# A feed-forward's second product by seven block products instead of eight, with its buffers moved and its gathers placed earlier in the loop

## The chip, the cores and the metric

The kernel runs on one core of one Trainium2 chip. TensorE (PE) multiplies, and loads its stationary operand with an instruction of its own (shown as PEld); VectorE (DVE), ScalarE (ACT) and GpSimd (POOL) do the element-wise work; SyncE (SP) issues most of the transfers, and POOL issues the indirect ones. Each engine works through its own queue in order. The metric is the device time of the core in microseconds (us), as the median of several runs. Beside it stands one profiled execution, from which all durations come.

## The reference

The input is one sequence of S = 4096 tokens of D = 256 features, in float32. It is normalised once, and the result goes two ways.

```python
xn = _layernorm(x)
x  = x + attn_block(xn) + experts(xn)

# attn_block: attention in windows of 64 with 8 heads, then
x = xn + attn;  x = _layernorm(x, gamma, beta)
h = gelu(x @ W1 + b1)            # W1: 256 x 1024
x = x + (h @ W2 + b2)            # W2: 1024 x 256

# experts: 8 experts with 816 hidden features, the best two of each token
h = silu((xf @ gw.T + gb) * (xf @ uw.T + ub))
acc = acc + w[:, None] * (h @ dw.T + db)
```

The change is in `h @ W2`, the feed-forward's second product.

## The kernel before

The constants are P = 128, D = 256, F1 = 1024, FC1 = F1 / P = 8, G = 512 tokens in a group, NG = 8 groups, TG = 4 tiles of 128 tokens in a group, B = 256. Everything is float32. For TensorE, PE, DVE, ACT, POOL and SP the order of work is the order in which the code is written: nothing reorders it.

The kernel has three stretches. First the tokens are normalised, projected and routed to experts. Then 34 expert units, of two tiles of tokens or one, run in a loop whose first 32 turns also carry the attention; five further units follow that run only if the routing has need of them (`whole`, L890). Each unit's results go to a table in DRAM, `done`. In the third stretch, from L1267 to the end, the feed-forward runs over eight groups of 512 tokens. In the profiled execution it begins near 867 us.

For a group g the third stretch has these steps:

- `second_loads` (L1040): SP loads the attention's output `x2` and the input `acc`, each 128 x 1024.
- `second_norm` (L1047): DVE normalises `x2` (four instructions at L1051) and multiplies by gamma (L1059); POOL adds beta to `x2` (L1060), `b2` to `acc` (L1061) and `x2` to `acc` (L1062).
- `turned2` (L1064): PE transposes `x2` with eight instructions (L1069); DVE copies the two results to `x2T` (L1072).
- `hidden` (L1075): 16 products with 512 moving columns (L1080), two for each of eight chunks f; ACT applies gelu with the bias (L1087) and writes the tile `hT` of 128 x 8 x 512.
- `picked` (L1090): POOL issues eight indirect gathers (L1096), for four tiles of tokens the results of two experts each, from `done` into eight buffers `got`.
- `combined` (L1105): DVE adds each gathered tile to `acc`, times the token's share (L1109): eight instructions.
- `second` (L1113): 32 products with 256 moving columns (L1118), each summing over the eight chunks f; DVE adds the results to `acc`, two tiles at once (L1125).
- `store` (L1128): SP writes `acc` to the output (L1129).

A product in float32 is two MATMUL instructions with a weight load ahead of each, so a group's `hidden` has 32 MATMULs in the profile, and its `second` has 64. The stationary operand of `second` is a 128 x 128 piece of `hT`, and the moving one a row of `W2`.

The loop from L1273 sets the order. In the turn of g: `hidden(g)`, `turned2(g + 1)`, loads and `second_norm(g + 2)`, `second(g - 1)`, `combined(g - 1)`, `store(g - 1)`, `picked(g)`. After the loop come `combined(7)`, and `second(7)` with a store after each half. PSUM has seven banks in turn (`bank`, L124; `psm`, L115); `ph`, `pt`, `pd` all draw on it.

SBUF is dealt out from two sides as a stack. On the left lie the constants, and the experts' pools `wexp` (L113) and `he` (L789), which are kept to the end. On the right, the attention's pools are given back at L1184, and in their place come `wf` (the weights), `hf` (x2T and hT, two buffers each), `accp`, `got`, and `late` (what the last five units need: gathered tokens, their transposes, two sets of weights).

## Time and profile before

| | |
|---|---|
| three runs, us | 1101.41, 1103.53, 1105.42 (median 1103.53) |
| profiled execution, us | 1102.41 |
| its span, first to last instruction, us | 1100.7 |
| granted TensorE clock | 1.000 of full speed |
| busy: PE, PEld, DVE, ACT, POOL, us | 1084.8, 868.7, 591.3, 495.3, 502.7 |
| L1118 MATMUL (`pd`), 128x256, x512 | 111.7 us in all |
| L1080 MATMUL (`ph`), 128x512, x256 | 111.3 us in all |
| L1069 MATMUL (`pt`), 128x128, x64 | 8.3 us in all |

How to read it: "busy" is the time in which at least one instruction of the engine was under way. MATMULs are pipelined, so the mean length of one (379 ns for `pd`) is more than the distance from one to the next; the distance is a stretch's length over its count. A share of busy time over the whole kernel mixes stretches with different limits; the change touches the third one, which is looked at by itself. The profiled execution's device time is 1.7 us above its span.

### The profile page before, as it was taken

How to read it: one execution, taken by the hardware profiler on the slowest of the kernel's cores; microseconds unless marked ns; L12 is line 12 of the kernel's file. 1: busy time of each engine (PE TensorE's matmuls, PEld its weight loads, DVE VectorE, ACT ScalarE, POOL GpSimd, SP SyncE). 2: the span in 40 equal slices, each digit the busy share in tenths (PEclk: the TensorE clock that was granted, in tenths of full speed). 3: DMA queues.
4: the chain of work that ended last, by engine and by line, in shares of the span. 5: the costliest groups of instructions: out<-in, count | busy, mean ns of one | idle time of the engine just before them, and what ended most of it. 6: DMA issues, size and time to landing. Idle time of an engine off the chain costs nothing. (4 is left out here: it accounts for less than half of the span.)

```text
span 1100.7 us, 18039 instructions
## 1 busy us (share of the span) xinstructions
PE 1084.8 (99%) x6424; PEld 868.7 (79%) x6424; DVE 591.3 (54%) x1571; ACT 495.3 (45%) x1170; POOL 502.7 (46%) x620
## 2 busy tenths in 40 slices
PE   8998999999999999999999999999999999999998
PEld 6577888887888888888888888888888666666667
DVE  6655656657566566665666666656433233323213
ACT  4526446544555546646555564465343321111110
POOL 6425544455445443654455445534213175555422
PEclk9999999999999999999999999999999999999999
DMA  9152445545445354454544554545575323333112
GB/s 291 61 234 73 139 136 172 180 141 156 152 147 194 119 187 148 170 163 155 193 149 138 179 182 140 169 150 197 176 265 205 120 77 96 96 96 96 57 58 77
DMA packets 60748, 163.37 MB, mean 148 GB/s; under 512 B 6288, under 2 KB 46608, under 8 KB 51184
## 3 DMA queue, kind: packets, MB, share of 16 engines
q1 hardware_dynamic: 54176, 144.48, 37.7%
q0 software_dynamic: 6480, 17.70, 6.2%
q8 instruction: 52, 0.85, 0.3%
q14 instruction: 40, 0.33, 0.1%
HBM read 140.28 MB, written 21.89 MB: 147 GB/s over the span
## 5 line engine op out<-in xcount | busy, mean ns | idle before, releaser
L830 PE MATMUL gu<-xsT,wg 128*128 128x256 f32 (+1 forms) x1632 | 357.4, 369 | 0.7 <-ACT xsT L822 0.7
L830 PEld LDWEIGHTS gu<-xsT,wg 128*128 128x128 f32 x1632 | 288.6, 190 | 46.2 <-DVE oT L1018 10.3
L838 ACT ACTIVATE gs<-gu,wg 128x256 f32<-128x256 f32 (+1 forms) x204 | 92.1, 454 | 291.3 <-PE gu L830 290.0
L958 POOL TENSOR_TENSOR pr<-pr 128x256 f32<-128x256 f32 x128 | 92.9, 726 | 253.6 <-ACT pr L946 253.6
L874 PE MATMUL pe<-wd,hT 128*128 128x256 f32 x896 | 199.0, 379 | 0.0
L839 DVE SCALAR_TENSOR_TENSOR hT<-gu,wg,gs 128x256 f32<-128x256 f32 (+1 forms) x204 | 95.0, 467 | 177.4 <-ACT gs L838 177.2
L874 PEld LDWEIGHTS pe<-wd,hT 128*128 128x128 f32 x896 | 170.1, 190 | 22.8
L959 POOL TENSOR_TENSOR pr<-pr,ident 128x256 f32<-128x256 f32 x128 | 126.2, 986 | 10.0
L946 ACT ACTIVATE pr<-pr,nm 128x256 f32<-128x256 f32 x256 | 126.8, 498 | 0.4
L1087 ACT ACTIVATE hf<-ph,b 128x512 f32<-128x512 f32 x64 | 44.0, 687 | 158.2 <-PE ph L1080 158.2
L1080 PE MATMUL ph<-x2T,W 128*128 128x512 f32 x256 | 111.3, 593 | 0.8 <-DVE x2T L1072 0.8
L1118 PE MATMUL pd<-W,hf 128*128 128x256 f32 x512 | 111.7, 379 | 0.0
L1118 PEld LDWEIGHTS pd<-W,hf 128*128 128x128 f32 x512 | 96.9, 190 | 13.3 <-issue 0.5
L931 DVE CUSTOM_DVE_ANT_0 pr<-ps,mask 128x256 f32<-128x256 f32 x256 | 90.8, 420 | 23.2 <-PE ps L917 23.2
L804 POOL DMA_INDIRECT xs<-xnd,token x71 | 68.8, 969 | 64.9 <-DVE paired_tiles L771 31.1
L1096 POOL DMA_INDIRECT got<-done,slot x64 | 63.3, 989 | 73.9 <-DVE acc L1109 61.2
L1080 PEld LDWEIGHTS ph<-x2T,W 128*128 128x128 f32 x256 | 48.5, 190 | 58.9 <-issue 56.8
L869 ACT ACTIVATE hT<-hT 128x512 f32<-128x512 f32 (+3 forms) x148 | 80.4, 543 | 7.6 <-DVE hT L839 4.2
L1060 POOL TENSOR_TENSOR x<-x,beta 128x1024 f32<-128x1024 f32 x8 | 18.8, 2350 | 94.4 <-DVE x L1059 94.4
L1125 DVE TENSOR_TENSOR acc<-pd,acc 128x512 f32<-128x512 f32 x16 | 11.0, 690 | 83.3 <-PE pd L1118 83.3
L978 DVE TENSOR_TENSOR pr<-pr,rec 128x1024 f32<-128x1024 f32 x32 | 39.2, 1225 | 27.7 <-POOL pr L958 27.7
L946 ACT ACT_TABLE_LOAD x31 | 39.8, 1283 | 27.5 <-DVE nm L931 27.5
(209 smaller groups left out, 1393.6 us busy)
## 6 DMA issues: line engine op xcount, KB each, us to landing
wg<-in_gate_up SPq DMA_DIRECT2D x37, 1670.5 KB, 7.1
wd<-in_down SPq DMA_DIRECT2D x37, 1024.0 KB, 5.9
done<-y SPq DMA_DIRECT2D x30, 256.0 KB, 2.2
x<-in_x SPq DMA_DIRECT2D x8, 512.0 KB, 5.6
xnd<-xn SPq DMA_DIRECT2D x8, 512.0 KB, 5.4
res<-xnd SPq DMA_DIRECT2D x16, 256.0 KB, 2.9
x1d<-res SPq DMA_DIRECT2D x16, 256.0 KB, 2.2
x<-x1d SPq DMA_DIRECT2D x8, 512.0 KB, 5.8
```

Of the source, the lines that this page charges most:

```text
L804: nc.gpsimd.indirect_dma_start(out=x[:, t, :], out_offset=None, in_=xnd, in_offset=bass.IndirectOffsetOnAxis(ap=token[:, i : i + 1], axis=0),)
L830: nc.tensor.matmul(pb[:, k, :], w[:, lo : lo + P], xT[:, c, :], start=(c == 0), stop=(c == DC - 1),)
L838: nc.scalar.activation(gs, pb[:, 0, :], AF.Identity, bias=w[:, gb : gb + 1])
L839: nc.vector.scalar_tensor_tensor(hT[:, f, :], pb[:, 1, :], w[:, ub : ub + 1], gs, ALU.add, ALU.mult)
L869: nc.scalar.activation(hT[on, lo:hi, :], hT[on, lo:hi, :], AF.Silu)
L874: nc.tensor.matmul(pd[:, t, :], hT[:, f, t * P : (t + 1) * P], w[:, f * D : (f + 1) * D], start=(k == 0), stop=(k == FCE - 1),)
L931: nc.vector.tensor_tensor_reduce(out=pr[:, hh, j, :], in0=ps[hh][:, j, :], in1=mask[:, kind + j, :], scale=-1.0, scalar=-LOWEST, op0=ALU.a ...
L946: nc.scalar.activation(pr[:, hh, j, :], pr[:, hh, j, :], AF.Exp, bias=nm[:, j, hh : hh + 1], scale=-1.0, accum_out=sums[:, j, hh : hh + 1],)
L958: nc.gpsimd.tensor_tensor(first, first, second, ALU.add)
L959: nc.gpsimd.tensor_tensor(second, second, bcast(ident, 2, 1), ALU.mult)
L1080: nc.tensor.matmul(ph, W1[:, c, f * P : (f + 1) * P], x2T[:, c, :], start=(c == 0), stop=(c == DC - 1),)
L1118: nc.tensor.matmul(pd[:, u, :], hT[:, f, (t + u) * P : (t + u + 1) * P], W2[:, f, :], start=(f == 0), stop=(f == FC1 - 1),)
```

## The change

`second` is rewritten. Per group the hidden matrix is a 512 x 1024 matrix and W2 is 1024 x 256; each is cut in two along both sides, into A11..A22 (256 tokens x 512 hidden features) and B11..B22 (512 x 128 features). In place of eight block products, seven are formed, of sums of blocks. Each product has two tiles of tokens, four chunks f and 128 moving columns.

- Sums of W2's blocks: `sums_of_weights`, four POOL instructions, once, into a new tile `V2` (in turn 33 of the unit loop).
- Sums of the hidden blocks: `sums_of_hidden`, per group one POOL instruction and three on DVE, of 128 x 1024 each, into a new tile `hv`.
- The products' results are added to quarters of `acc`, on DVE, by way of a small tile `u` that holds partial sums; ACT copies the first product into it.
- The turn's order is changed: `combined(g - 1)` comes right after `hidden(g)`, `picked(g)` before the products, the sums of the hidden blocks after the second product, loads and `second_norm(g + 2)` after the fifth, the store at the turn's end.
- `wexp`, `he` and `late` are given back after the last unit, and `hf` and `got` are made then, in their place. `late` thus lies directly after `accp` before that.

```diff
-    wexp = pool(ctx, "wexp", bufs=2)
+    experts_done = ctx.enter_context(ExitStack())
+    wexp = pool(experts_done, "wexp", bufs=2)
...
-    he = pool(ctx, "he", bufs=2)
+    he = pool(experts_done, "he", bufs=2)
...
+    FH = FC1 // 2
+    F_LO, F_HI = slice(0, FH), slice(FH, FC1)
+    C1, C2 = slice(0, P), slice(P, D)
+
+    def sums_of_weights():
+        b11, b12, b21, b22 = W2[:, F_LO, C1], W2[:, F_LO, C2], W2[:, F_HI, C1], W2[:, F_HI, C2]
+        t1, t2, t3, t4 = (V2[:, k] for k in range(4))
+        for out_, left_, right_ in ((t1, b12, b11), (t2, b22, t1), (t3, b22, b12), (t4, b21, t2)):
+            nc.gpsimd.tensor_tensor(out_, left_, right_, ALU.subtract)
+
+    def sums_of_hidden(g, hT):
+        v = hf.tile([P, 4, FH, B], F32, tag="hv", name=f"hv{g}")
+        a11, a12, a21, a22 = hT[:, F_LO, 0:B], hT[:, F_HI, 0:B], hT[:, F_LO, B:], hT[:, F_HI, B:]
+        s1, s2, s3, s4 = (v[:, k] for k in range(4))
+        nc.gpsimd.tensor_tensor(s3, a11, a21, ALU.subtract)
+        nc.vector.tensor_tensor(s1, a21, a22, ALU.add)
+        nc.vector.tensor_tensor(s2, s1, a11, ALU.subtract)
+        nc.vector.tensor_tensor(s4, a12, s2, ALU.subtract)
+        return v
...
-    def second(g, acc, hT):
-        for t in range(0, TG, 2):
-            pd = halves(bank(f"pd{g}_{t}"))
-            for u in range(2):
-                for f in range(FC1):
...
-            nc.vector.tensor_tensor(acc[:, t : t + 2, :], pd, acc[:, t : t + 2, :], ALU.add)
-            yield t
+    def second(g, acc, hT, v):
+
+        t1, t2 = slice(0, 2), slice(2, 4)
+        u = hf.tile([P, 2, P], F32, tag="u", name=f"u{g}")
+
+        def product(n, left, right):
+            pb = bank(f"s{g}_{n}").rearrange("p (t n) -> p t n", n=P)[:, 0:2]
+            for t in range(2):
+                for f in range(FH):
                     nc.tensor.matmul(
+                        pb[:, t, :],
+                        left[:, f, t * P : (t + 1) * P],
+                        right[:, f, :],
                         start=(f == 0),
+                        stop=(f == FH - 1),
                     )
+            return pb
+
+        def add(t, cols, pb):
+            nc.vector.tensor_tensor(acc[:, t, cols], pb, acc[:, t, cols], ALU.add)
+
+        p1 = product(1, hT[:, F_LO, 0:B], W2[:, F_LO, C1])
+        nc.scalar.copy(u, p1)
+        add(t1, C1, u)
+        yield
+        p2 = product(2, hT[:, F_HI, 0:B], W2[:, F_HI, C1])
+        add(t1, C1, p2)
+        yield
+        p6 = product(6, v[:, 1], V2[:, 1])
+        nc.vector.tensor_tensor(u, p6, u, ALU.add)
+        add(t1, C2, u)
+        yield
+        p5 = product(5, v[:, 0], V2[:, 0])
+        add(t1, C2, p5)
+        add(t2, C2, p5)
+        yield
+        p7 = product(7, v[:, 2], V2[:, 2])
+        nc.vector.tensor_tensor(u, p7, u, ALU.add)
+        add(t2, C1, u)
+        add(t2, C2, u)
+        yield
+        p3 = product(3, v[:, 3], W2[:, F_HI, C2])
+        add(t1, C2, p3)
+        yield
+        p4 = product(4, hT[:, F_HI, B:], V2[:, 3])
+        add(t2, C1, p4)
+        yield
...
-            hf = pool(ctx, "hf", right, bufs=2)
             accp = pool(ctx, "accp", right, bufs=4)
-            got = pool(ctx, "got", right, bufs=8)
+            V2 = wf.tile([P, 4, FC1 // 2, P], F32, tag="V2", name="V2")
...
-            late = pool(ctx, "late", right)
+            late = pool(late_done, "late", right)
...
         if b == STEPS + 1:
+            sums_of_weights()
...
+    late_done.close()
+    experts_done.close()
+    hf = pool(ctx, "hf", right, bufs=2)
+    got = pool(ctx, "got", right, bufs=8)
     x2T = turned2(0, x2s[0][1])
     second_norm(1, *x2s[1])
...
     for g in range(NG):
         hT = hidden(g, x2T)
+        if g > 0:
+            acc = x2s.pop(g - 1)[0]
+            combined(g - 1, acc, ys)
         if g + 1 < NG:
             x2T = turned2(g + 1, x2s[g + 1][1])
+        ys = picked(g)
+        outs = second(g - 1, acc, *last) if g > 0 else iter(())
+        some(outs, 2)
+        last = hT, sums_of_hidden(g, hT)
+        some(outs, 3)
         if g + 2 < NG:
             x2s[g + 2] = second_loads(g + 2)
             second_norm(g + 2, *x2s[g + 2])
+        some(outs, 2)
         if g > 0:
-            acc = x2s.pop(g - 1)[0]
-            list(second(g - 1, acc, before))
-            combined(g - 1, acc, ys)
             store(g - 1, 0, TG, acc)
-        before = hT
-        ys = picked(g)
     acc = x2s.pop(NG - 1)[0]
     combined(NG - 1, acc, ys)
-    for t in second(NG - 1, acc, before):
-        store(NG - 1, t, 2, acc)
+    outs = second(NG - 1, acc, *last)
+    some(outs, 6)
+    store(NG - 1, 0, 2, acc)
+    some(outs, 1)
+    store(NG - 1, 2, 2, acc)
```

More of the change, by code (lines that the diff above doesn't have):

```diff
@@ L1111, in combined @@
             )
-    def second(g, acc, hT):
-        for t in range(0, TG, 2):
-            pd = halves(bank(f"pd{g}_{t}"))
-            for u in range(2):
-                for f in range(FC1):
+    def second(g, acc, hT, v):
[5 more added lines that the diff above has]
+                for f in range(FH):
                     nc.tensor.matmul(
-                        pd[:, u, :],
-                        hT[:, f, (t + u) * P : (t + u + 1) * P],
-                        W2[:, f, :],
+                        pb[:, t, :],
+                        left[:, f, t * P : (t + 1) * P],
+                        right[:, f, :],
                         start=(f == 0),
-                        stop=(f == FC1 - 1),
+                        stop=(f == FH - 1),
                     )
-            nc.vector.tensor_tensor(acc[:, t : t + 2, :], pd, acc[:, t : t + 2, :], ALU.add)
-            yield t
+            return pb
[27 more added lines that the diff above has]
+        yield
     def store(g, t, n, acc):
@@ L1141, in block_kernel @@
     flags = {}
+    late_done = ctx.enter_context(ExitStack())
     def load_unit(b):
@@ L1267, in block_kernel, with some @@
     x2s[1] = second_loads(1)
+    late_done.close()
+    experts_done.close()
+    hf = pool(ctx, "hf", right, bufs=2)
+    got = pool(ctx, "got", right, bufs=8)
     x2T = turned2(0, x2s[0][1])
     second_norm(1, *x2s[1])
-    before = None
+    last = None
+    def some(steps, n):
+        for _ in range(n):
+            next(steps, None)
     for g in range(NG):
         hT = hidden(g, x2T)
+        if g > 0:
+            acc = x2s.pop(g - 1)[0]
+            combined(g - 1, acc, ys)
         if g + 1 < NG:
             x2T = turned2(g + 1, x2s[g + 1][1])
+        ys = picked(g)
[3 more added lines that the diff above has]
+        some(outs, 3)
         if g + 2 < NG:
```

## The prediction

> **What bounds it now.** I read the summary first, then the chain of work that ended last in order of time, then the stretch it lies in.
>
> ```profile
> PE 1084.8 (99%) x6424; PEld 868.7 (79%) x6424; DVE 591.3 (54%) x1571; ACT 495.3 (45%) x1170; POOL 502.7 (46%) x620
> ```
>
> PE is never idle for long, so time is won only by giving PE less to do. The chain (start us, us, what) shows a loop that is PE alone:
>
> ```profile
> 858.65 5.36 PE whole L830 x48
> ...
> 912.23 13.73 PE ph L1080 x32
> 925.96 0.87 PE pt L1069 x8
> 926.84 13.82 PE pd L1118 x64
> 940.65 13.73 PE ph L1080 x32
> ...
> 1096.03 0.06 DVE acc L1125
> ```
>
> A turn is 13.73 + 0.87 + 13.82 = 28.4 us, without a gap. How full the other engines are in one turn is shown by the busy times of this stretch (length, then PE, PEld, DVE, ACT, POOL, clock, DMA share, GB/s):
>
> ```profile
> 926.80:954.40 27.60, 27.60 (x99) 18.27 (x98) 8.34 (x17) 4.81 (x7) 14.95 (x11) 1.00 0.31 96
> ```
>
> DVE and ACT have two thirds of a turn free, POOL nearly half.
>
> **The products.** Before, `pd` is 64 MATMULs of 256 columns in 13.82 us: 215.9 ns each. After, there are 7 products x 2 tiles x 4 chunks x 2 instructions = 112 MATMULs of 128 columns. Columns fall to 7/8, but each MATMUL still has its own weight load, so loads rise from 64 to 112 a group. The nearest row is the last conditional unit, where 48 MATMULs of just this shape follow each other (durations in ns: min/median/max):
>
> ```profile
> L830 PEld LDWEIGHTS whole<-xsT,wg x48: 191/192/193, 858.4 to 863.6; 128*128 128x128 f32 x48
> L830 PE MATMUL whole<-xsT,wg x48: 274/275/276, 858.5 to 863.7; 128*128 128x128 f32 x48
> ```
>
> The chain gives these 48 as 5.36 us: 111.7 ns each, although one load is recorded as 192 ns; so loads and MATMULs overlap, and the record's length isn't the price. A group costs 112 x 0.1117 = 12.51 us, which saves 1.31 us, and over eight groups **10.5 us**. The lower bound of a MATMUL's price is the transposes, 8 in 0.87 us = 108.8 ns, nearly what half of 215.9 gives: 12.2 us a group, 13 us saved. For the upper one, a fresh bank for each product may cost up to 0.06 us, half a MATMUL: 12.9 us a group, 7.2 us saved.
>
> A rule speaks against this. The Trainium skill, "TensorE: Matmul & The Clock Gate", section "The mechanism", says that a weight load overlaps matmuls in flight only where the row group differs; here all 128 rows are the same. With that page's load price ("LDWEIGHTS", columns over 1.2 GHz: 107 ns) on top of 108.8 ns, a group is an estimated 112 x 0.216 = 24.2 us, 83 us more in all. But then `pd` would now need 64 x (107 + 213) ns = 20.5 us and not 13.82. I take the row.
>
> **DVE.** Its prices, and POOL's:
>
> ```profile
> L1059 DVE TENSOR_TENSOR x<-x,gamma 128x1024 f32<-128x1024 f32 x8 | 9.8, 1225 | 0.3
> L907 DVE TENSOR_TENSOR xs<-whole,wd 128x256 f32<-128x256 f32 x2 | 0.8, 425 | 4.5 <-PE whole L874 2.3 <-PEq L1262 2.3
> L1060 POOL TENSOR_TENSOR x<-x,beta 128x1024 f32<-128x1024 f32 x8 | 18.8, 2350 | 94.4 <-DVE x L1059 94.4
> L1096 POOL DMA_INDIRECT got<-done,slot x64 | 63.3, 989 | 73.9 <-DVE acc L1109 61.2 <-issue 12.5
> ```
>
> Removed: two adds of 128x512, 1.38 us. Added: three sums at 1.225 = 3.68 us, eleven adds of 128x256 at 0.425 = 4.7 us. DVE goes from 8.4 to about 15.4 us in a turn of 27.1: still hidden. Counted from a turn's start T (its `hidden`): `combined` runs from T + 1.4 to 5, the copies of `turned2` at T + 14.2, the sums T + 18.6 to 22.3, gamma ends at T + 27.7, the last add at T + 28.5. What PE needs first of these are the x2T copies (by T + 27.1, ready at T + 15.5) and the banks: `ph` of the next turn takes the bank of the third product at T + 35.7, whose add ends at T + 28.1. No PE wait. Without this cover each late us of DVE would cost a us, but 7 are spare.
>
> **ACT.** One copy of 128x256, 0.37 us as in the row of that shape at L304, without a table load (L304 has none). Hidden: ACT idles 15 us while `pd` runs.
>
> **POOL and the moved gathers.** Eight gathers took 10.06 us (893.95 to 904.01) whether early or late in the turn. With s3 at 2.35 us and three adds of `second_norm` POOL has 10.1 + 4 x 2.35 = 19.5 us in 27.1. In steady state the gathers run from T + 7.7 to 17.8, s3 to 20.2, and beta waits for gamma at T + 27.7, ready long before the `turned2` that needs it, at T + 40.8. `picked` is now queued ahead of s3 and `second_norm`; it waits for `combined(g - 1)`, finished by T + 5, so nothing stands behind it for long. The loads on SP come before the store as queued, and `x2` lands about T + 8, needed at T + 25. The four sums of W2 cost 4 x 1.27 us (L1024's 128x512 row) near 803.4, where POOL is idle until 828.04. All hidden.
>
> **One place is not hidden**: the first turn. There `picked(0)` and s3 now stand before the beta of `second_norm(2)`:
>
> ```profile
> 880.11 2.36 POOL L1062 TENSOR_TENSOR acc<-acc,x 128x1024 f32<-128x1024 f32 x1
> ...
> 896.95 0.14 PEld L1069 LDWEIGHTS pt<-ident,x 128*128 128x128 f32 x1 [0.24 <-issue]
> ```
>
> POOL is free at 882.5. The gathers end at 892.6, s3 at 895.0, beta at 897.4, where PE wants `x2(2)` for its transposes at 896.95. To this comes that POOL is held up by DVE instructions with two SBUF inputs:
>
> ```profile
> 773.87 1.23 DVE L978 TENSOR_TENSOR pr<-pr,rec 128x1024 f32<-128x1024 f32 x1 [1.39 <-POOL pr L958]
> ...
> 773.91 1.76 POOL L959 TENSOR_TENSOR pr<-pr,ident 128x256 f32<-128x256 f32 x1
> ```
>
> (0.72 us elsewhere); a gather beside L1059 took 1.28 in place of 0.95 us. The three sums and gamma stretch the gathers by 4 x 0.33 us: beta ends about 898.9, and PE waits **+1.5 us**, once (0 with no stretch; +3.5 if every DVE sum holds POOL for its whole length). The Trainium skill, "SBUF — State Buffer", section "Who interferes with whom", goes further than the row: whichever of the two starts first blocks the other, so a POOL add of 2.35 us can hold DVE too, which no row here shows. In a turn that is at most four POOL adds, 9.4 us later for DVE: `combined` then ends at T + 39 instead of 32, before the next x2T copies at T + 41.3. Either way the sum stays.
>
> **Memory given back.** `hf` takes the place of `late`, whose last tile is stored to `done` at 867.62, landing 2.2 us later; x2T(0) was written at 867.51. If x2T lies over that tile, the start slips by 2.3 us; over weights or transposes, by 0, as PE's reads are over. `hT` over it costs nothing (gelu begins at 870.28, and seven banks buffer it). `late` is made in the order weights, tokens, so I take 0 and keep 2.3 for the range.
>
> **The tail.** Now PE ends at 1095.70, DVE is still at `combined(7)` because its gathers waited for `combined(6)`; the two adds end at 1097.22, the last store is issued, and the span ends 3.5 us later. After, `combined(7)` is over long before, and after PE's end one add of 0.425 us remains: 0.45 + 3.5 instead of 5.0: **-1.1 us** (-0.5 to -1.5).
>
> **Sum**: -10.5 + 1.5 - 1.1 = -10.1 us. Span 1100.7 - 10.1 = 1090.6; with 1.7 us around it, 1092.3. The profiled execution lies 1.1 us under the median of the runs shown, which would give 1093.4; I put the forecast between, **1092.9**.
>
> **Rivals.** (a) *Weight loads set the pace*, chance 0.07. A load recorded as 192 ns is longer than the 109 ns of MATMUL that must cover it; with hT and acc traffic it might not be covered as in the row. Break-even is 13.82 / 112 = 123 ns a MATMUL; from 128 ns the kernel is slower by over 0.3%. At the recorded 192 ns: 21.5 us a group, +61 us, about 1163. Against: 48 in 5.36 us with PEld busy throughout. (b) *POOL becomes the bound*, 0.06. Its 19.5 us plus all of DVE's two-input work in a turn (gamma 1.2, sums 3.7, adds of `u` 1.7, `combined` 3.9) is 30.0 us against 27.1; six turns give +17 us less some 8 us of lead: about no change, 1102. Against: half of that DVE work falls where POOL waits. (c) *Small waits*: x2T(0) behind the store and a longer first wait, or 0.4 us in each group: 1095 to 1099, chance 0.12. (d) *Nothing is saved because something else ends last*: excluded by a chain that is PE in every turn. The forecast has 0.75.
>
> **From cases to numbers.** 0.3% is 3.3 us, about what this kernel's measurement can tell from no change. Faster: forecast, (c), and a part of (b), 0.88. Same: 0.03 from (b). Slower: (a) and the rest of (b), 0.09. Low end: 13 us from the products, no first wait, tail -1.5: about 1089. High end: products 7.2, first wait 3.5, slip 2.3, tail -0.5 leaves -1.9; not all together, so 1099, which holds (c).
>
> **What would show it.** Right: a group's seven products as 112 MATMULs in 12.5 us, directly after `pt`; PE without idle except near 897 us, then waiting for POOL's beta; after PE's last MATMUL one add. Wrong: gaps of PE between products that wait for DVE (banks) or POOL (s3); a distance of MATMULs above 120 ns; x2T(0) waiting for a transfer.

## The result, and the profile after

The changed kernel took 1098.85 us (median of 9 runs, 1096.73 to 1100.21) beside 1103.05 us (9 runs, 1101.41 to 1105.42) for the kernel before: a ratio of 0.996, 95% interval [0.9948, 0.9972]. It is faster by 4.2 us, where 10.1 us had been predicted; the time, 1098.85 us, lies just inside the range given. The profiled execution of the changed kernel took 1100.01 us with a span of 1098.3 us, so it is read against the 1100.7 us of before: 2.4 us less.

The engines' summary of the profile after. PE has more instructions and 4.7 us less to do, DVE 100 us more:

```profile
PE 1080.1 (98%) x6808; PEld 873.9 (80%) x6808; DVE 691.6 (63%) x1667; ACT 498.1 (45%) x1178; POOL 528.4 (48%) x632
```

The chain that ended last, in order of time (start us, us, what), shows where the gain is and where it went:

```profile
901.53 12.51 PE s L1150 x112
914.04 13.73 PE ph L1081 x32
...
984.24 0.87 PE pt L1070 x8
985.11 7.04 PE s L1150 x63
992.14 0.14 issue
992.29 0.68 PE s L1150 x4
992.97 0.72 issue
993.69 5.29 PE s L1150 x45
998.98 13.73 PE ph L1081 x32
...
1069.58 25.03 PE s L1150 x224
1094.61 0.02 issue
1094.63 0.42 DVE acc L1160
```

In the first turn the seven products take the 12.51 us that were predicted, and the last two groups take 25.03 us. But in the turns between them PE stops inside the products ("issue": it waits for nothing that the profile shows). From the first MATMUL of `s` to the first of the next `ph`, these five turns take 13.52, 13.72, 13.87, 14.12 and 13.53 us, together 6.2 us above 5 x 12.51; some of that lies inside the pieces, whose single records aren't all there. The two timelines of the turn at 985 us show what runs beside it (start us, us, engine, line, operation, idle time before it); first POOL, from the first gather to s3:

```profile
982.28 0.98 POOL L1124 DMA_INDIRECT got<-done,slot  x1
...
991.39 0.94 POOL L1124 DMA_INDIRECT got<-done,slot  x1 [0.30 <-issue]
992.35 2.36 POOL L1112 TENSOR_TENSOR hv<-hf 128x1024 f32<-128x1024 f32 x1
```

Then DVE, with the adds of the first and the second product:

```profile
987.34 0.42 DVE L1160 TENSOR_TENSOR acc<-u,acc 128x256 f32<-128x256 f32 x1 [1.34 <-ACT u L1163]
992.27 0.43 DVE L1160 TENSOR_TENSOR acc<-s,acc 128x256 f32<-128x256 f32 x1 [4.51 <-remote]
```

A product takes 1.79 us, so the second one, begun 1.79 us after 985.11, was done at 988.7. Its add starts at 992.27, 3.6 us later, though DVE idles in front of it. The eighth gather ends at 992.33; within 0.1 us the signal of the second product has arrived and PE, which stopped at 992.14, goes on for four MATMULs, then stops for 0.72 us more. In the other four turns the same add starts 2.7, 3.1, 2.6 and 3.6 us after its product is done, and PE's stops lie between 2.4 us before and 1.5 us after the end of the last gather. So where a row of gathers runs beside the products, PE's signals come late, and PE itself stops.

The third stretch as a whole, from the first `ph` to PE's end, took 227.4 us before (868.26 to 1095.70) and takes 223.2 us (871.38 to 1094.61): -10.5 from the products, +6.2 from these stops; PE's first wait for POOL added nothing in this execution (from that first `ph` to the first product it is 30.15 us in both).

The stretch also begins 3.1 us later. Of this, 1.7 us is one piece of 3.41 us at half the granted clock, at 94.5 us, which this profile has and the profile of before has not (the mean clock is 0.998 here, 1.000 there). 1.65 us is lost in the last attention unit, where PE shows the same kind of stop (16 MATMULs take 5.37 us and not 3.72):

```profile
787.12 0.97 PE L831 MATMUL gu<-xsT,wg 128*128 128x256 f32 x2
788.44 1.19 PE L831 MATMUL gu<-xsT,wg 128*128 128x256 f32 x3 [0.35 <-issue]
789.85 2.64 PE L831 MATMUL gu<-xsT,wg 128*128 128x256 f32 x11 [0.22 <-issue]
```

and again a row of gathers ends just then, at 788.40 us; this is the last of seven, which fetch the conditional units' tokens:

```profile
787.46 0.94 POOL L805 DMA_INDIRECT xs<-xnd,token  x1 [0.30 <-issue]
```

In the kernel before these seven ran from 794.86 to 803.35 us, because the place of `late` made them wait for the attention's store of `res` to `x1d`:

```profile
794.86 0.99 POOL L804 DMA_INDIRECT xs<-xnd,token  x1 [17.02 <-DMA x1d<-res]
```

In the changed kernel they run from 779.91 to 788.40.

At the end one add is left after PE, as forecast: 1098.3 - 1094.61 = 3.7 us, 5.0 before. Sum against the span of before: -10.5 + 6.2 + 3.1 - 1.3 = -2.5 us, against -2.4 measured.

### The profile page after: what moved, and what is told of

It is laid out like the page before. It is cut to its first block, busy times and chain, and to the rows that moved or that the text cites. A ratio compares the mean times of both kernels' runs of the same rounds, so it can differ in the third digit from the quotient of the medians.

```text
span 1098.3 us, 18954 instructions
## 1 busy us (share of the span) xinstructions
PE 1080.1 (98%) x6808; PEld 873.9 (80%) x6808; DVE 691.6 (63%) x1667; ACT 498.1 (45%) x1178; POOL 528.4 (48%) x632
## 5 line engine op out<-in xcount | busy, mean ns | idle before, releaser
L1137 DVE SCALAR_TENSOR_TENSOR acc<-got,share,acc 128x256 f32<-128x256 f32 x64 | 66.7, 1072 | 1.1
L980 DVE TENSOR_REDUCE same<-pr 128x8 f32<-128x1024 f32 x32 | 39.1, 1221 | 19.8 <-POOL pr L960 19.8
L1150 PE MATMUL s<-V,hv 128*128 128x128 f32 x384 | 46.5, 276 | 3.7 <-issue 3.4
```

What stands on the lines that cost most here:

```text
L1150: nc.tensor.matmul(pb[:, t, :], left[:, f, t * P : (t + 1) * P], right[:, f, :], start=(f == 0), stop=(f == FH - 1),)
```

## The experiments

They ran on five chips, called A to E here; the kernels of one chip share their runs of the kernel before. Which chip gave the result is not on record. The chips turned out to matter, so the table names them. "Stops" is the time by which the stretches of the second product in turns 1 to 5 exceed 5 x 12.51 us (5 x 13.82 with eight products), by the profile. "First ph" is the start of the third stretch. Both are of one execution, which need not be a typical one: e1's profile took 1110.73 us and e8's 1099.77 us, each several us above the median of its runs. Pieces at half the granted clock also move "First ph", by up to 1.7 us each.

| kernel | chip | median, us | ratio to before [95%] | stops, us | first ph, us |
|---|---|---|---|---|---|
| changed (result) | - | 1098.85 | 0.9960 [0.9948, 0.9972] | 6.2 | 871.4 |
| e1, changed | A | 1104.76 | 1.0007 [0.9991, 1.0024] | 6.9 | 876.0 |
| e2, `got` made first | A | 1105.43 | 1.0015 [0.9999, 1.0030] | 7.2 | 875.2 |
| e3, gathers last | A | 1109.76 | 1.0055 [1.0037, 1.0073] | 7.1 | 872.1 |
| e4, memory alone | A | 1107.47 | 1.0027 [1.0020, 1.0033] | 0 | 874.3 |
| e9, changed | B | 1098.10 | 0.9951 [0.9932, 0.9970] | 2.8 | 872.2 |
| e6, gathers first | B | 1099.58 | 0.9968 [0.9956, 0.9980] | 0.6 | 870.9 |
| e7, e6 and old place | B | 1097.37 | 0.9948 [0.9935, 0.9961] | 1.0 | 868.0 |
| e8, eight gathers | B | 1095.00 | 0.9921 [0.9907, 0.9935] | 0 | 876.3 |
| e5, `late` in old place | C | 1097.53 | 0.9947 [0.9929, 0.9964] | 4.2 | 869.6 |
| f1, gathers beside eight | C | 1102.36 | 0.9989 [0.9981, 0.9998] | 0 | 869.2 |
| f2, pairs | C | 1102.31 | 0.9993 [0.9981, 1.0004] | 0 | 873.3 |
| f3, pairs and old place | C | 1100.10 | 0.9971 [0.9959, 0.9983] | 0 | 868.8 |
| f4, pairs from turn 1 | D | 1092.91 | 0.9902 [0.9887, 0.9918] | 0 | 868.1 |
| f5, fours | D | 1093.72 | 0.9913 [0.9897, 0.9930] | 0 | 868.3 |
| f6, plain, SyncE | D | 1092.17 | 0.9896 [0.9880, 0.9911] | 0 | 869.1 |
| f7, plain, GpSimd | D | 1092.21 | 0.9897 [0.9880, 0.9913] | 0 | 869.7 |
| g1, changed | E | 1093.52 | 0.9916 [0.9902, 0.9929] | 0 | 870.1 |
| g2, plain, GpSimd | E | 1092.04 | 0.9907 [0.9892, 0.9922] | 0 | 869.7 |

### Chip A: the place of the gathers, and the memory alone

**e1**, the changed kernel as it is.

> The changed kernel itself, a second time. In its first profile, PE stood still for about 1 to 1.6 us inside the seven products of each of turns 1 to 5 (6.2 us in all), and for 1.65 us in unit 32; the completion signals of the second, third and fourth product came 1.6 to 4.4 us late, while POOL issued gathers. Theory G (gathers beside the products hold PE's signals up): the same waits in the same turns, 5 to 7 us in all, and a ratio to the kernel before of 0.996. Theory R (those waits belonged to that one execution): fewer than 2 us of waits in the products in this profile, or waits in other turns; the product stretches of turns 1 to 5 then take 12.5 us each, as in turns 0, 6 and 7.

On this chip the gain is gone: 1.0007 [0.9991, 1.0024], with 6.9 us of stops in turns 1 to 5, 2.8 more in turn 0, and 1.85 us of recorded waits in the last attention unit. Pieces of 3.41 us at half the granted clock stand right behind two of these places (at 792.0 and 921.7 us), so that a stop is paid once more: the `ph` after the second one takes 15.25 us and not 13.73.

**e2**, the gathers' buffers made in another place.

```diff
             accp = pool(ctx, "accp", right, bufs=4)
+            got = pool(ctx, "got", right, bufs=8)
...
     hf = pool(ctx, "hf", right, bufs=2)
-    got = pool(ctx, "got", right, bufs=8)
```

> The changed kernel with one line moved: the gathers' eight buffers are made at their place of before, between the accumulators and the late units' pool, so their address in SBUF is another one; order of work unchanged. Theory M (the gathers' new place in memory makes them disturb PE): the products' waits in turns 1 to 5 vanish, about 6 us gained on the changed kernel, ratio 0.991 to the kernel before. Theory G (what counts is that gathers run beside products): the same 5 to 7 us of waits and the same ratio, 0.996.

The stops stay (7.2 us) and so does the time. So the new place of the gathered rows isn't the cause.

**e3**, gathers and their sums at the end of the turn.

```diff
-            combined(g - 1, acc, ys)
...
-        ys = picked(g)
         outs = second(g - 1, acc, *last) if g > 0 else iter(())
...
         if g > 0:
+            combined(g - 1, acc, ys)
             store(g - 1, 0, TG, acc)
+        ys = picked(g)
```

> The changed kernel with the placing of the gathers and of their use undone: as in the kernel before, the gathered results are added after the products, then the store, then the next gathers, at the turn's end. The gathers then run beside the next turn's hidden products (512 columns) for the most part, and the seven products have few gathers beside them. Theory G: PE's waits in the products fall from about 6 us to under 1.5 us; against it stands the end, where the last gathers wait again for the adds of turn 6 (about 1 us later than in the changed kernel): a ratio of 0.992 to 0.993. Theory L (DVE and POOL, which block each other when both read SBUF, are what holds PE up): waits stay at 4 us or more, ratio 0.996 or above.

This was meant to take the gathers away from the products, and didn't. They wait for `combined`, which now comes late and is itself held up beside POOL's adds (9.46 us for eight sums that took 3.9 before), so that the gathers again lay beside the products: in one turn from 955.5 to 965.5 us, with products from 959.1. The stops were the same, 7.1 us. The tail grew besides: after the last group's gathers all its sums and adds were still to come. One thing is new: here the last group's gathers (1086.93 to 1097.24) lie beside its products, where no other kernel has gathers, and PE stops there too, for 0.25 and 0.45 us, before it waits for the late sums.

```profile
1096.44 0.27 PE L1150 MATMUL s<-W,hv 128*128 128x128 f32 x1 [0.25 <-issue]
```

The stops go where the gathers go, but the run frees hardly any products of gathers and so doesn't show the cause.

**e4**, the kernel before, with eight products and its old order, and only the memory given back as in the change.

```diff
-    wexp = pool(ctx, "wexp", bufs=2)
+    experts_done = ctx.enter_context(ExitStack())
+    wexp = pool(experts_done, "wexp", bufs=2)
...
-    he = pool(ctx, "he", bufs=2)
+    he = pool(experts_done, "he", bufs=2)
...
-            hf = pool(ctx, "hf", right, bufs=2)
...
-            got = pool(ctx, "got", right, bufs=8)
...
-            late = pool(ctx, "late", right)
+            late = pool(late_done, "late", right)
...
+    late_done.close()
+    experts_done.close()
+    hf = pool(ctx, "hf", right, bufs=2)
+    got = pool(ctx, "got", right, bufs=8)
```

> The kernel before with the memory part alone: experts' buffers and late buffers given back before the third stretch, the hidden tiles and the gathers' buffers made then; eight products, old order. In the changed kernel the seven gathers of the late units ran at 780 to 788 us, beside the last attention unit, instead of 795 to 803, and PE stood still for 1.65 us there. If the memory's moving (late buffers come free earlier) causes that: the same early gathers and a wait of 1 to 2 us in unit 32, ratio 1.001 to 1.002. If it was chance: no wait there, ratio 1.000. If handing the memory back also delays the first hidden products, up to 2.3 us more.

The memory alone makes the kernel slower, by 0.27% [0.20, 0.33], 2.2 to 3.6 us. Its profile has the seven early gathers (779.96 to 788.46), two waits of PE of 1.00 and 1.03 us in the last attention unit, and a half-clock piece at 790.6. The second wait:

```profile
790.01 5.30 PE L831 MATMUL gu<-xsT,wg 128*128 128x256 f32 x16 [1.03 <-issue]
```

Its third stretch is unchanged, products of 13.8 us without a stop. So the late start of the third stretch comes with the memory. Whether the stops in the products do can't be seen here, since e4 keeps the eight products and the old order; e2 and e5 bear on that.

### Chip B: are gathers the cause?

**e9**, the changed kernel as it is.

> The changed kernel, to be read beside the three below on the same chip. It gave a ratio to the kernel before of 0.996 in one place and 1.0007 in another; PE's waits in the products of turns 1 to 5 were 6.2 and about 7 us, in unit 32 1.65 us and 1.85 us plus one stretch of 3.41 us at half clock. Expected: a ratio between 0.996 and 1.001, 5 to 8 us of waits in the products, a wait in unit 32.

Stops of 2.8 us, fewer than on A, and a ratio of 0.9951 [0.9932, 0.9970].

**e8**, the gathers of seven groups of eight left out. The sums of the later groups reuse the first group's gathered rows, so the kernel leaves out these groups' own experts' part; all other instructions stay.

```diff
-        ys = picked(g)
+        if g == 0:
+            ys = picked(g)
```

> The changed kernel without 56 of its 64 gathers in the third stretch: only the first group's results are gathered, and all groups add these, so the experts' part of the other groups is left out. Everything else as it is, the late pool too. Theory G: no waits of PE in the products of turns 2 to 5 (each stretch of seven products 12.5 us), 4 to 6 us less than the changed kernel. Theory L: DVE and POOL still block each other, the waits stay at 4 us or more. Theory D (the products' own rate of instructions holds PE up): the waits stay too.

Every product stretch is 12.51 us, though the sums on DVE, the other suspect, are slower than ever. First the costliest groups of this run (mean ns after the comma), then its chain:

```profile
L1137 DVE SCALAR_TENSOR_TENSOR acc<-got,share,acc 128x256 f32<-128x256 f32 x64 | 78.8, 1261 | 1.7 <-DMA got<-done,slot 0.6
```

```profile
988.85 12.51 PE s L1150 x112
1001.36 13.74 PE ph L1081 x32
1015.09 0.87 PE pt L1070 x8
1015.97 12.51 PE s L1150 x112
```

The third stretch is 218.0 us (876.34 to 1094.35), where the prediction's own terms give 227.4 - 10.5 + 1.5 = 218.4. Take the gathers out and the forecast's arithmetic holds; so what DVE and POOL do to each other isn't the cause, nor the pace of the MATMULs alone. Nor was it a run in which nothing stops: the stop in the last attention unit, whose seven gathers were left, is still there (0.35 and 0.93 us), and the half-clock piece at 793.1 us behind it.

**e6**, the same instructions, with two POOL adds of the second normalization moved behind the gathers, so that these start earlier in the turn.

```diff
         nc.gpsimd.tensor_tensor(x2, x2, bcast(beta, TG, 1), ALU.add)
+
+    def residual2(acc, x2):
         nc.gpsimd.tensor_tensor(acc, acc, bcast(b2, TG, 1), ALU.add)
...
         ys = picked(g)
+        if g + 1 < NG:
+            residual2(*x2s[g + 1])
```

> The changed kernel with the two POOL additions to the accumulator taken out of the second norm and placed after the gathers of the next turn, so that POOL reaches the gathers some 5 us earlier: T + 3 to T + 13 in place of about T + 11 to T + 21, beside the hidden products and not beside the seven products. The same instructions in all. Theory G (gathers beside the dense products hold PE's signals up): the waits in the products fall from 5 to 8 us to under 1.5 us, and the time by 5 to 7 us against the changed kernel. Theory L (DVE held by POOL's additions): DVE stays as late as before and the waits stay.

The stops fall from 2.8 to 0.6 us, as the gathers end 3.3 to 7.8 us into the products, in every turn sooner than in e9 (6.6 to 9.1 us). But in the first turn the moved adds hold DVE (four TENSOR_SCALARs take 8.20 us, 1.4 elsewhere), POOL's beta comes late, PE waits 2.1 us for it, and a half-clock piece follows. The time is no better than that of e9.

**e7**, e6 with a pad of 40 KB a partition below `late`, so that its tiles lie where they lay before.

```diff
+            pad = pool(late_done, "pad", right)
+            pad.tile([P, 10 * F1], F32, tag="pad", name="pad")
```

> The previous one, and 40 KB left empty ahead of the late units' pool, so that it lies where it lay in the kernel before and its seven gathers have to wait for the attention's last store again (795 to 803 us in place of 780 to 788). Theory: the wait in unit 32 (1.65 to 3.7 us with the half-clock stretch that it draws) is gone; 2 to 4 us less than the previous one, about 8 to 10 us less than the changed kernel, ratio 0.990 to 0.992 to the kernel before. Rival: the early gathers have nothing to do with unit 32, then no difference to the previous one.

The stop in the last attention unit is gone, and the third stretch starts at 868.03 us, as before the change (868.26) and 2.8 us earlier than in e6; but e6's profile also has a half-clock piece at 11.5 us that e7's lacks, and part of the 2.8 us may be due to that. The median falls by 2.2 us.

### Chip C: the place of `late`, dense and less dense work, pairs

**e5**, the changed kernel with this pad and nothing else.

> The changed kernel with a pad of 40 KB in the pool's stack, so that the tiles of `late` lie where they lay before; nothing else differs. Theory A (the move of `late` costs by itself: in its new place the seven gathers of the last units run some 15 us earlier, beside the last attention unit, and TensorE stops there): no stop of TensorE in the last attention unit, the third stretch begins near 868 us as before and not near 871 to 876, and the time is 2 to 4 us under the changed kernel's, a ratio to the kernel before of about 0.993 to 0.995. The products keep their waits (2 to 6 us over turns 1 to 5). Theory B (the late beginning of the third stretch comes from elsewhere, by chance of the clock): it begins near 871 to 876 us, and the time is the changed kernel's.

The seven gathers run from 796.39 again and the last attention unit has no stop. Its PE timeline in place of the three rows shown above:

```profile
787.10 3.72 PE L831 MATMUL gu<-xsT,wg 128*128 128x256 f32 x16
790.65 1.89 PE L1032 MATMUL wo<-Wo,oT 128*128 128x256 f32 x8
```

The third stretch starts at 869.64 us; the 1.4 us left against 868.26 are about what a half-clock piece at 93.5 us costs. The products keep 4.2 us of stops. So there are two causes, and they are separate: e5 has the second without the first, e8 the first without the second.

**f1**, eight products of 256 columns, old memory, with the sums and gathers put ahead of the products, so that the gathers run beside `pd`.

```diff
+        if g > 0:
+            acc = x2s.pop(g - 1)[0]
+            combined(g - 1, acc, ys)
+        ys = picked(g)
+        if g > 0:
+            list(second(g - 1, acc, before))
...
-            acc = x2s.pop(g - 1)[0]
-            list(second(g - 1, acc, before))
-            combined(g - 1, acc, ys)
...
-        ys = picked(g)
```

> The kernel before, eight products of 256 columns, its memory and its experts' order kept; only the order of the third stretch is changed: the sums of the gathered rows of the group before and the gathers of the next come ahead of the second product, and the second normalization's loads behind it, so that the gathers run beside the second product. Theory A (a series of gathers stops TensorE only where its stream of instructions is dense: 224 instructions in 12.5 us in the seven products, 128 in 13.8 us in the eight): the stretches of the second product stay at 13.8 us in all turns, with no wait above 0.3 us in them; the time is that of the kernel before, or about 1 us less at the end, where the last gathers no longer wait for the sums of the group before. Theory B (a series of gathers stops any product that it runs beside): the stretches of turns 1 to 6 are 14.5 to 16 us, and the time is 4 us or more above the kernel before.

In the turn at 984.66 us eight gathers run in a row from 986.21 to 996.29 us, all beside `pd`, and PE doesn't notice. First POOL's last one, then the chain:

```profile
995.34 0.94 POOL L1096 DMA_INDIRECT got<-done,slot  x1 [0.30 <-issue]
```

```profile
984.66 13.81 PE pd L1118 x64
998.47 1.72 PE ph L1080 x4
```

All turns are 13.81 or 13.82 us, and none of the kernel's 11 runs (1100.71 to 1104.81) is slower than the slowest of the kernel before (1105.89). So a row of gathers isn't enough; it takes these products beside it. What in them matters isn't shown, as the eight products also differ in columns, banks and adds. A likely reading is that PE's instructions stand closer together. The seven products issue 224 instructions (loads and MATMULs) in 12.51 us, 17.9 a microsecond; the eight issue 128 in 13.82 us, 9.3 a microsecond. In the last attention unit the stop follows 32 small MATMULs (128*32 weights, `po`) in 1.0 us, which is dense too. The kernel also gains 0.11% [0.02, 0.19]: its last gathers no longer wait, and from PE's end to the end of the span it is 4.0 us and not 5.0.

**f2**, e6 with the gathers in pairs, a POOL add between two pairs, and in the first turn the second normalization of group 2 ahead of the gathers. **f3** adds the pad.

```diff
+        if g == 0:
+            x2s[2] = second_loads(2)
+            second_norm(2, *x2s[2])
+        ys = []
+        gathers = picked(g, ys)
+        adds = residual2(*x2s[g + 1]) if g + 1 < NG else iter(())
+        for _ in range(3):
+            some(gathers, 2)
+            some(adds, 1)
...
         last = hT, sums_of_hidden(g, hT)
+        some(gathers, 3)
```

> The changed kernel with the next turn's gathers issued in pairs, one add of the second normalization on GpSimd between two pairs, and in the first turn the second normalization of group 2 ahead of the gathers; same instructions, other order on GpSimd. Theory A (it takes three or four gathers in a row beside the dense products to hold TensorE's completion signals back): the stretches of the second product are 12.5 to 12.8 us in all turns, the first product's wait for GpSimd near 900 us is gone, and the third stretch takes 218 to 220 us; with the late start of that stretch kept, the time is 1094 to 1097 us beside a kernel before at 1103.7, a ratio of 0.992 to 0.994. Theory B (any gather beside the dense products holds them, about 0.7 us each): the stretches of turns 1 to 5 are 13.5 us or more, as in the changed kernel.

> Both edits together: gathers in pairs, and the pad of 40 KB that keeps `late` in its old place. If both causes of the missing gain are right and independent, the third stretch begins near 868 us and takes 218 to 220 us, and the time is 1090 to 1093 us beside a kernel before at 1103.7, a ratio of 0.988 to 0.990, which is what was predicted for the change. If one of them is not the cause, the ratio is 0.992 or above.

In turns 1 to 5 both are as hoped: 12.51 us in each, on the chip where e5 stops for 4.2 us, and with gathers beside the products. That this execution wasn't one without stops is shown by f2 itself: in its last attention unit, beside the seven gathers in a row, PE stops as in the result.

```profile
788.22 0.38 PE L831 MATMUL gu<-xsT,wg 128*128 128x256 f32 x1 [0.85 <-issue]
788.92 0.47 PE L831 MATMUL gu<-xsT,wg 128*128 128x256 f32 x1 [0.32 <-issue]
```

Of f3, two gathers that start a pair, and the chain:

```profile
989.79 0.97 POOL L1126 DMA_INDIRECT got<-done,slot  x1 [0.16 <-issue]
...
994.55 0.97 POOL L1126 DMA_INDIRECT got<-done,slot  x1 [0.16 <-issue]
```

```profile
989.20 12.51 PE s L1152 x112
1001.70 1.72 PE ph L1084 x4
```

The times miss both expectations (0.9993 and 0.9971) by a fault of the edit in the first turn: the first gathers stand behind the second normalization there, `combined(0)` and the copies of x2T stand behind them on DVE, and PE waits 5.8 us for these copies before the sixth product. With seven banks in turn, that product takes the bank of `pt` again, which the copies must empty first. From f3:

```profile
913.76 3.79 PE L1152 MATMUL s<-W,hv 128*128 128x128 f32 x16 [5.85 <-DVE x2T L1076]
```

With the half-clock piece that follows (6.83 us at 912.7 in f3), some 9 us are lost in that stretch. The pad takes 2.2 us off here too (1102.31 to 1100.10). On this chip no kernel with pairs and a sound first turn was run.

### Chips D and E: another answer

**f4**, the eight gathers of the first turn ahead again, pairs from turn 1 on, with the pad; the lines below are against f3. **f5**, the same with rows of four.

```diff
-        if g == 0:
-            x2s[2] = second_loads(2)
-            second_norm(2, *x2s[2])
...
-        for _ in range(3):
-            some(gathers, 2)
-            some(adds, 1)
+        if g == 0:
+            some(gathers, 9)
+            x2s[2] = second_loads(2)
+            second_norm(2, *x2s[2])
+        else:
+            for _ in range(3):
+                some(gathers, 2)
+                some(adds, 1)
...
         some(gathers, 3)
+        some(adds, 3)
```

> As the run with pairs and the old place of `late`, but in the first turn the eight gathers go first, then the second normalization of group 2, then the adds on GpSimd; pairs from the second turn on. If the two causes are the whole of the missing gain: the third stretch begins near 868 us, every stretch of the second product takes 12.5 us, TensorE's wait for GpSimd near 900 us stays under 0.5 us, TensorE ends near 868.2 + 218 = 1086.5 us, the span is near 1090 us and the time 1090 to 1093 us, a ratio of 0.988 to 0.990 to the kernel before at 1103.7. If something else is still lost: 1095 us or more, ratio 0.992 or above.

> The same kernel with the gathers in two rows of four from the second turn on, two adds of GpSimd between. Theory length (it takes about four in a row beside the dense products before signals are held): waits of 0.1 to 0.8 us in some turns, time 1091 to 1095 us. Theory any gap (any gap of some microseconds lets the signals catch up): no wait, time as with pairs. If the place were what counts and not the row's length, waits of 0.7 to 1.5 us a turn in the turns in which the second four fall on the first half of the products.

f4 took 1092.91 us, 0.9902 [0.9887, 0.9918]: first `ph` at 868.07, all products 12.51 us, PE's end at 1086.15, span 1089.8, all as expected. f5 has no stop in the products either. The causes named so far would have it that the pairs did this; the last runs take that proof away.

**f6** and **f7**, the changed kernel with plain loads of the same bytes in place of the gathers.

```diff
-                nc.gpsimd.indirect_dma_start(
-                    out=y,
...
+                nc.sync.dma_start(out=y, in_=done[(2 * i + k) * P : (2 * i + k + 1) * P, :])
```

> The changed kernel with each gather replaced by a plain load of 128 consecutive rows of the experts' outputs, issued by SyncE: same bytes into the same tiles, no indices. Left out: the picking of each token's own rows, so the experts' part is of other tokens. Theory traffic (the rows' landing beside the products holds TensorE): waits of 3 to 7 us over turns 1 to 5 as in the changed kernel. Theory GpSimd (what it takes GpSimd to issue a gather, 0.95 us each, back to back, holds TensorE): product stretches of 12.5 us in all turns.

> The same plain loads, issued by GpSimd in place of SyncE; the picking is left out in the same way. Theory indices (it is the indirect form, a transfer of one row each, that holds TensorE): product stretches of 12.5 us in all turns. Theory issuing (any row of transfers issued by GpSimd back to back does it): waits of 2 us or more over turns 1 to 5.

Both run without any stop, at 0.990. Taken alone this would say that only gathers by index stop PE. But the stop in the last attention unit was gone as well, although its seven gathers by index were there at the same time as in the result (779.91 to 788.40 in f7). No theory here says that; so the chip itself came under suspicion. The changed kernel hadn't run on it.

**g1**, the changed kernel as it is, and **g2**, f7 again, on one further chip.

> The changed kernel once more, to be read beside the kernel with plain transfers on the same chip. If it stops in the last attention unit and in the products (2 to 7 us over turns 1 to 5), the chip is one that shows the stops, and the other run's verdict counts. If it shows none (product stretches of 12.5 us, third stretch from 869 us, time near 1092 us, ratio 0.990), the stops belong to some chips only, and the run with plain transfers on its first chip tells nothing of its cause.

> The kernel with plain loads of 128 consecutive rows issued by GpSimd in place of the third stretch's gathers, once more (the picking of each token's own rows is left out). The seven gathers in the last attention unit are those of the changed kernel. Theory chip (the first run was on a chip without stops): the stop in the last attention unit is there, 0.6 to 2 us, if the changed kernel beside it has one. Theory indices (only series of gathers by index hold TensorE): product stretches of 12.5 us in all turns where the changed kernel has 13 us or more. Theory issuing: waits of 2 us or more over turns 1 to 5 here too.

The changed kernel, with no edit at all, takes 1093.52 us here, 0.9916 [0.9902, 0.9929], without a stop; all its five runs (1091.86 to 1094.70) lie below the fastest of the result (1096.73). Its chain, and POOL's last gather and DVE's add of the second product in the same turn as above:

```profile
982.61 12.51 PE s L1150 x112
995.12 13.73 PE ph L1081 x32
...
1063.09 25.03 PE s L1150 x224
1088.11 0.02 issue
```

```profile
987.12 1.48 POOL L1124 DMA_INDIRECT got<-done,slot  x1 [0.30 <-issue]
```

```profile
986.23 0.42 DVE L1160 TENSOR_TENSOR acc<-s,acc 128x256 f32<-128x256 f32 x1 [0.96 <-PE s L1150]
```

The eight gathers run in a row from 978.15 to 988.60 us, 6.0 us into the products that begin at 982.61 (in the result's execution they ran 7.2 us into them). The second product, done at 982.61 + 3.57 = 986.18, has its add at 986.23, in the middle of the gathers: nothing is held back. That the gathers lie a little earlier is not the reason: in the turn at 928.38 us they run 8.6 us into the products, without a stop, and in e5 on C 8.7 us into those at 929.05, with 1.0 us of stops. The seven gathers in the last attention unit run from 780.22 to 788.72, and the 16 `gu` MATMULs at 787.42 take 3.72 us without a gap. With nothing to remove, f6, f7 and g2 can't say what in a gather causes the stops; on D the changed kernel itself wasn't run, but the seven untouched gathers say the same of that chip. The test of plain loads decides nothing, and whether f4 keeps its time on A, B or C is not shown.

## Why the prediction was right or wrong

**The products: right.** 112 MATMULs take 12.51 us in every turn in which PE doesn't stop, in all kernels and on all chips, so eight groups save 10.5 us. The row of 48 MATMULs of the last conditional unit was the price, and the rule about the overlap of weight loads, weighed against it, doesn't hold for this kernel: two instructions every 111.7 ns, all with full rows. (The section that the prediction names also lets a load into the background weight buffer go ahead, which the prediction left out; no run here tells whether it is that.) Rival (a) is out.

**"POOL and the moved gathers ... All hidden": this step failed.** The working asked only when POOL is done and who waits for it. That the gathers, moved ahead of the products, would run *beside* PE's densest stream wasn't looked at, and they took 6.2 of the 10.5 us back in the profiled execution. The profile names no releaser for these stops. e8 against e9 (no gathers, no stops), f1 (gathers beside 256-column products, no stops) and f2 and f3 against e5 (the same gathers in pairs, no stops) show that it is the row of gathers beside these products, on the chips that stop at all. By which path a gather does it stays open. Rival (c), "0.4 us in each group", had the size, 1095 to 1099, but not the mechanism.

**"Memory given back ... I take 0": this step failed too.** It considered only what `hf` is laid over. What moved time was `late`: in its new place its gathers are released 15 us earlier, beside the last attention unit, and PE stops there for 1.65 us. e4 shows a loss of 2.2 to 3.6 us with the memory alone, e5 and e7 that the stop goes with the place. The slip of 2.3 us that was kept for the range had another reason, so that it covers this loss in size is luck.

**On one chip the number was right.** On E the third stretch of the unchanged changed kernel is 218.0 us (870.11 to 1088.11), by the prediction 218.4, with a first wait of +1.0 us where +1.5 was predicted; the span of 1091.8 us is within 0.5 us of the predicted 1090.6 and 1.7 us for a half-clock piece at 93.9 us; the time of 1093.52 us stands beside the predicted 1092.9. Elsewhere the ratio of the changed kernel went from 0.995 to 1.0007. So the failed step was to hold that the moved gathers cost nothing; how much they cost depends on the chip or on what else ran at that time, and that could not be read from one profile.

**The first wait: bounded right.** POOL's beta ended at 900.28 us (about 898.9 forecast, in a stretch that began 3.1 us later). The prediction's own terms add up to 898.6 and not 898.9, so to +1.2 and not +1.5 us. In the result's execution PE lost nothing by it, on E 1.0 us.

**DVE and POOL: right, more than was priced.** The hold of DVE by POOL, which the rule in the Trainium skill, "SBUF — State Buffer", section "Who interferes with whom", states and no row of before showed, is real: the sums of gathered rows went from 482 to 1072 ns on average, and a sum of hidden blocks, at 992.62 us, took 3.18 us and not 1.23 with POOL's s3 beside it. "Either way the sum stays" held: e8 has the slowest sums and the best stretch. In e6 and f2, where DVE was next to the path in the first turn, the same hold did cost PE time. One need was overlooked: the sixth product takes the bank of `pt`, so the x2T copies are wanted near T + 14.6 + 5 x 1.79 = T + 23.5 and not T + 27.1. In the changed kernel they are in time; in f2 and f3 they were not, and PE waited 5.8 us.

**The tail: right**, -1.3 us for -1.1. Rival (b) is out: POOL never ended last in steady state.

## What to carry to other kernels

When a step is moved, ask not only who waits for it but what it will run beside: on three of these chips a row of indexed gathers stopped PE beside seven products of 128 columns (17.9 PE instructions a microsecond), and on one of the three it was free beside eight of 256 (9.3). Give memory back with an eye to every tile that moves by it, since a buffer that comes free earlier starts transfers earlier. And before an absence is taken for the effect of an edit, run the unedited kernel on the same chip: here the stops had vanished by themselves.

## What was unexpected of the hardware

- While eight gathers run in a row beside dense MATMULs, the end of a product reaches DVE up to 3.6 us late (add at 992.27 for a product done at 988.7), and PE stops for 0.1 to 0.8 us at a time. With pairs, and a POOL add (2.36 us) between two of them, PE doesn't stop on the same chip (f2, f3 beside e5). By which path a gather does this is open.
- It depends on the chip or on what else ran at that time: 6.2 us in the result, 6.9, 2.8 and 4.2 us (the last with the pad) on A, B and C, none on E, and no sign of it on D. All of them ran the kernel before within 1102.4 to 1104.3 us.
- After some stops of a microsecond or two the granted clock was one half for 3.41 us, e.g. at 792.0 us after waits of 1.10 and 0.75 us in e1; after others, such as 0.98, 0.35 and 0.34 us in e3 (787.3 to 789.7), it was not. Such a piece costs PE 1.7 us, so that 1.85 us of waits cost 3.6.
